# A graph layer on one core: x W1b + b1 read from a table in DRAM, both silus in one operation, source addresses made once and kept in DRAM, x once in SBUF, 72 and 76 columns a step

## The chip, the cores and the metric

The kernel runs on one core of a Trainium2 chip. A core has TensorE (PE), VectorE (DVE), ScalarE (ACT), GpSimd (POOL) and SyncE (SP), each with an instruction stream of its own, and sixteen DMA engines that they share. The streams meet at semaphores only. The metric is device time in microseconds, from the first to the last instruction of one execution and the little around it; the result is compared in runs of both kernels on the same chip.

An engine's stream is walked by its sequencer. It hands instructions to the engine, and carries out register loads (TENSOR_LOAD), semaphore instructions and DMA issues by itself. The profile counts only the engine's own work as busy.

## What is computed

One message-passing layer on a graph with 12,500 nodes of 64 features and 400,000 edges with 16 features. The edges are sorted by destination.

```
m_in = concatenate([x[src], x[dst], edge_attr])          # 400000 x 144
h = silu(m_in @ W1 + b1)                                 # 400000 x 64
messages = silu(h @ W2 + b2)                             # 400000 x 64
agg = segment_sum(messages, dst, 12500)                  # 12500 x 64
out = layernorm(x + silu(concatenate([x, agg]) @ W3 + b3))
```

W1 is used in three parts: W1a for x[src], W1b for x[dst], W1c for the edge features. All numbers are float32.

## The kernel before

**Tiles and steps.** Edges go in tiles of 128, eight tiles to a step ("oct"). There are 3125 tiles and NO = 391 steps (the loop at line 601 runs over o). TensorE packs two tiles, a pair, side by side: 64 features of one on partitions 0 to 63 and of the other on 64 to 127. The loop is emitted under a manual schedule, so the order of PE, ACT, DVE and SP is the order in which the lines are written. GpSimd's gathers are scheduled by their buffers alone, three steps ahead (AHEAD) with five buffers.

**x[src] W1a.** For the first 12 steps (RAW) GpSimd gathers rows of x. In these steps a table pa = x W1a is made in DRAM (`table`), and from then on GpSimd gathers its rows: one indirect DMA a tile (line 373), and an identity matmul turns each pair of gathered tiles and adds them to PSUM (line 454). Not every tile is gathered by GpSimd. There are two other ways:

- *Columns* (`columns`, lines 271 to 300). x lies transposed in SBUF (xs, 64 features by nodes, a copy in each half of the partitions). For some pairs, those at the steps in the list `pairs`, each edge's column of four bytes on 64 partitions is copied into a tile cx of 128 columns, and a matmul with w1d multiplies it (line 451). ScalarE copies ACOLS = (32, 28) columns a step and VectorE VCOLS = (32, 32), by a reduction over one element. The addresses are loaded into the engine's registers before (line 290), 16 at the start of each of the two parts and then 8 at a time, cut at tile borders. A pair takes 256 columns, and it spares GpSimd the first two gathers of its step.
- *Rows* (`rows`, line 324). SP issues 16 DMAs a step, each of one row of pa, into a tile rx. A tile pair is complete every 16 steps.

The addresses of columns come by a DMA of 256 indices of src (`index`, line 351, three steps ahead, three buffers cxi) and two operations of VectorE that turn them into byte addresses (`address`, line 359), one a half, since the two halves of xs differ in address.

**x[dst] W1b and edge features.** Edges of a tile go to at most 48 nodes in a row, a window (S = 48). SP loads the window of x for step o + 3 (line 392), TensorE multiplies it by W1b (`window_product`, line 397), VectorE writes it into one of three tiles xw by a mask (`window_copy`, line 402). The tile's last 32 rows hold W1c. VectorE compares destinations with node numbers (`compare_dst`, line 424, 96 rows of oh), below which the edge features lie, and one matmul of xw with oh adds both (line 441).

**The two layers.** `first_layer` ends with a silu of ScalarE over 128x512 with b1 as bias (line 458). `second_layer` of the step before adds b2 by a matmul of three rows, multiplies by W2 and ends with another silu (line 473). The columns of ScalarE stand in two parts ahead of the two silus. `add_up` (line 482) multiplies the messages by the comparison eh (`compare_nodes`, line 430), and `add_window` (line 487) of VectorE adds the result into agg, four steps later. A node group's end, W3, layernorm and store, is spread over the steps (`later`).

**VectorE's order in step o:** the window bases (every fourth step), add_window(o - 4), compare_dst(o + 1), its first 32 columns, window_copy(o + 1), compare_nodes(o + 1), its second 32 columns, now and then the address operations or parts of the node groups.

**SP's order in step o:** index(o + 3), the rows' index (every 16 steps), the destinations and edge features of the next three steps (every third step), the window for o + 3, then the 16 rows. A DMA that waits holds back those behind it.

Of the kernel before, what the change touches and what calls it, by code (L numbers as in the profile page):

```python
# [28 lines left out]
RAW = 12  # L29
TABLES = 7  # L30
ACOLS = (32, 28)
VCOLS = (32, 32)
ROWS = 16
LOADS = (16, 8)
XBASE = (0, 64 << 18)
XADDR = 36864
# [7 lines left out]
@with_exitstack  # L44
def kernel(
    ctx: ExitStack,
    tc: tile.TileContext,
    x: bass.AP,
    xt: bass.AP,
    src_c: bass.AP,  # L50
    src_row: bass.AP,
    dst_c: bass.AP,
    dst_row: bass.AP,
    attr_t: bass.AP,
    dst_2: bass.AP,
    attr_2: bass.AP,
    base: bass.AP,
    w1: bass.AP,
    b1: bass.AP,
    w2: bass.AP,  # L60
    b2: bass.AP,
    w3: bass.AP,
    b3: bass.AP,
    out: bass.AP,
    edges: int,
):

    nc = tc.nc
    N, D = x.shape  # L80

    const = ctx.enter_context(tc.tile_pool(name="const", bufs=1))
    dram = ctx.enter_context(tc.tile_pool(name="dram", bufs=1, space=DRAM))
    pa = dram.tile([N, D], F32, name="pa")
    badi = const.tile([1, 1], I32, name="badi")
    ident = const.tile([P, P], F32, name="ident")
    make_identity(nc, ident)

    with ExitStack() as inner:
        windows(inner, tc, ident, badi, pa, x, xt, src_c, src_row, dst_c, dst_row, attr_t, dst_2, attr_2, base, w1, b1, w2, b2, w3, b3, out, edges)  # L90

    flag = nc.values_load(badi[0:1, 0:1], min_val=0, max_val=2 * P,
                          skip_runtime_bounds_check_because="a count of partitions")
    with tc.If(flag > 0):
        general(tc, ident, x, xt, src_c, dst_c, dst_row, attr_t, w1, b1, w2, b2, w3, b3, out, edges)


def windows(ctx, tc, ident, badi, pa, x, xt, src_c, src_row, dst_c, dst_row, attr_t, dst_2, attr_2, base, w1, b1, w2, b2, w3, b3, out, edges):
# [33 lines left out]
    b1s = const.tile([P, 1], F32, name="b1s")  # L132
# [3 lines left out]
    for s in range(2):  # L136
        h = slice(s * D, (s + 1) * D)
        nc.scalar.dma_start(w1d[h, h], w1[0:D, :])
        nc.scalar.dma_start(b1s[h, :], b1.rearrange("(k o) -> k o", o=1))
# [3 lines left out]
    def resident(s, c):  # L143
        w = min(XC, NP - c)
        nc.scalar.dma_start(xs[s * D:(s + 1) * D, c:c + w], xt[:, c:c + w])

    resident(0, 0)
# [3 lines left out]
    resident(0, XC)  # L151
# [41 lines left out]

    bf = fast.tile([1, NO], F32, name="bf")
# [10 lines left out]
    nc.vector.memset(mask[:, :D], 0.0)  # L205
    nc.vector.memset(mask[:, D:], 1.0)
# [29 lines left out]
    for k in range(3):  # L236
        t = fast.tile([P, P], F32, name=f"xw{k}")
        nc.vector.memset(t, 0.0)
        for q in range(2):
            nc.sync.dma_start(t[E + q * A:E + (q + 1) * A, q * D:(q + 1) * D], w1[2 * D:2 * D + A, :])  # L240
        xw.append(t)
# [6 lines left out]
    with tc.tile_pool(name="gat", bufs=AHEAD + 2) as gat, tc.tile_pool(name="drp", bufs=2) as drp, \  # L248
# [4 lines left out]
            tc.tile_pool(name="ps2", bufs=2, space=PSUM) as ps2, \  # L253
# [17 lines left out]
        def columns(o, eng, part):  # L271
            if o < RAW:
                return
            lo = (o - RAW) * RATE
            if eng == ENG.Activation:
                lo, n = lo + sum(ACOLS[:part]), ACOLS[part]
            else:
                lo, n = lo + sum(ACOLS) + sum(VCOLS[:part]), VCOLS[part]
            hi, todo = lo + n, n
            while lo < hi:  # L280
                j, e0 = lo // (2 * P), lo % (2 * P)
                if j >= len(pairs):
                    return
                n = min(hi - lo, P - e0 % P, LOADS[lo > hi - todo])
                if pairs[j] not in cols:
                    cols[pairs[j]] = cx.tile([P, P], F32, name="cx")
                t = cols[pairs[j]].bitcast(U8)
                s = e0 // P
                h = slice(s * D, (s + 1) * D)
                _, regs = nc.values_load_multi_w_load_instructions(  # L290
                    indices[j][0:1, e0:e0 + n], engines=(eng,), min_val=XBASE[s] + XADDR,
                    max_val=XBASE[s] + XADDR + 4 * (N - 1), skip_runtime_bounds_check_because="src names a node")
                for e, r in zip(range(e0 % P, e0 % P + n), regs):
                    to, frm = t[h, 4 * e:4 * e + 4], xb[h, ds(r - (XBASE[s] + XADDR), 4)]
                    if eng == ENG.DVE:

                        nc.vector.tensor_reduce(to, frm[:, :, None], AX.X, OP.max)  # L297
                    else:
                        nc.scalar.copy(to, frm)  # L299
                lo += n  # L300
# [46 lines left out]
        def index(o):  # L347
            for j in begun(o):
                t = cxi.tile([1, 2 * P], I32, name="cxi")
                e = octs[pairs[j]][1] * P  # L350
                nc.sync.dma_start(t, src_row[:, e:e + 2 * P])
                indices[j] = t

        def address(o):
            for j in begun(o):
                t = indices[j]
                for s in range(2):
                    h = slice(s * P, (s + 1) * P)
                    nc.vector.tensor_scalar(t[:, h], t[:, h], 4.0, float(XBASE[s] + XADDR), op0=OP.mult, op1=OP.add)

# [25 lines left out]

        def window_load(o):
            if o % 4 == 0:
                bases(ENG.SP, o)
            xr = win.tile([D, 2, S], F32, name="xr")  # L390
            frm = xt[:, ds(winreg.pop((ENG.SP, o)), S)]
            nc.sync.dma_start(xr, frm[:, None, :].to_broadcast([D, 2, S]))
            winrow[o] = xr

        def window_product(o):
            pw = mis.tile([P, P], F32, name="mm")
            nc.tensor.matmul(pw[:E, :], winrow[o].rearrange("k s w -> k (s w)"), w1bb.rearrange("k s m -> k (s m)"),  # L397
                             start=True, stop=True)
            winrow[o] = pw

        def window_copy(o):
            nc.vector.tensor_tensor(xw[o % 3][:E, :], winrow.pop(o)[:E, :], mask[:E, :], op=OP.mult)  # L402

        def load(c, o0=0, o1=CT // OT):
# [6 lines left out]
            for k in range(2):  # L411
                nc.sync.dma_start(dr[k * S:(k + 1) * S, e], dst_2[k:k + 1, d].to_broadcast([S, e.stop - e.start]))
            nc.sync.dma_start(oh[E:, e], attr_2[:, d])

        hots = {}
# [18 lines left out]
        def first_layer(o):  # L434
# [5 lines left out]
            p1 = ps1.tile([P, OT // 2, P], F32, name="p1")  # L440
            nc.tensor.matmul(p1[:, :k], xw[o % 3], oh, start=True, stop=False, skip_group_check=True)  # L441
            if o < RAW:
# [4 lines left out]
                xg = work.tile([P, OT // 2, P], F32, name="m")  # L447
# [8 lines left out]
            columns(o, ENG.Activation, 0)  # L456
            h = work.tile([P, OT // 2, P], F32, name="h")
            nc.scalar.activation(h[:, :k], p1[:, :k], AF.Silu, bias=b1s)  # L458
            made[o] = h, eh

        def second_layer(o):
# [3 lines left out]
            h, eh = made.pop(o)  # L465
            p2 = ps2.tile([P, OT, D], F32, name="p2")
# [4 lines left out]
            columns(o + 1, ENG.Activation, 1)  # L471
            m = work.tile([P, OT, D], F32, name="m")
            nc.scalar.activation(m[:, :n2], p2[:, :n2], AF.Silu)  # L473
            made[o] = m, eh

        def add_up(o):
            c, t0, n, first, last = octs[o]
            m, eh = made.pop(o)
# [114 lines left out]
        tables = list(range(0, N, 8 * P))  # L593
        cuts = [SCT] + [min(t + 46 * OT, TILES) for t in range(SCT, TILES, 46 * OT)]
# [3 lines left out]
        with tc.manual_schedule(engines={ENG.PE, ENG.Activation, ENG.DVE, ENG.SP}):  # L598
            compare_dst(0)
            compare_nodes(0)  # L600
            for o in range(NO + 1):
# [3 lines left out]
                for k in parts[3 * o - 3:3 * o] if o else []:  # L605
                    n = min(XC, NP - k)
                    nc.scalar.activation(agg[:, k:k + n], zero.to_broadcast([P, n]), AF.Copy)
                if o < 2:
                    for c in parts[2:5] if o == 0 else parts[5:]:
                        resident(0, c)  # L610
# [10 lines left out]
                if 5 <= o < 5 + (len(parts) + 1) // 2:  # L621
                    for c in parts[(o - 5) * 2:(o - 4) * 2]:
                        resident(1, c)
# [10 lines left out]
                if o + 1 < NO:  # L634
                    window_product(o + 1)
# [7 lines left out]
                if o < NO:  # L643
                    first_layer(o)
                if o == 0:
                    nc.vector.tensor_copy(b2r, b2p[:, None, :].to_broadcast([3, OT, D]))
                if o + 1 < NO:
                    window_copy(o + 1)
# [11 lines left out]
                if o >= 1:  # L660
                    for c in tables[(o - 1) * per:o * per]:
                        table(c)
                if o >= 2:
                    add_up(o - 2)
                if o >= 1:
                    second_layer(o - 1)
                address(o + 2)
# [297 lines left out]
```

## Time and profile before

| | |
|---|---|
| median of 10 runs | 3433.37 us (3429.05 to 3437.4) |
| profiled execution, time | 3431.88 us |
| its span, first to last instruction | 3429.6 us |
| PE busy | 2567.5 us (75%) |
| DVE busy | 2513.8 us (73%) |
| ACT busy | 2724.4 us (79%) |
| POOL busy | 2566.8 us (75%) |
| granted clock of TensorE | 0.769 |

No engine is at 90%, and in the 40 slices of the span all four stand at 7 or 8 tenths from the third slice to the last but one. Busy shares alone don't say which engine sets the time. A row of the costliest groups reads: line, engine, operation, what it writes and reads, count; busy us and mean ns of one; then the idle time just before, and what ended most of it. "issue" there means that the engine waited for nothing that the profile shows: its sequencer was doing something else. The mean of a short instruction is longer than the distance to the next, since one begins before the other has ended.

In the chain of waits that ended last only the last 110 us are covered, so it does not tell of the steady part.

### The profile page before, as it was taken

To read this page: it belongs to the slowest core of one execution; us is meant where nothing else is said; L and a number is where in the kernel's file an instruction comes from. 1 tells how busy PE (TensorE), PEld (TensorE's weight loads), DVE (VectorE), ACT (ScalarE), POOL (GpSimd) and SP (SyncE) were. 2 spreads that over 40 slices of the span, in tenths; PEclk is the share of its full clock that TensorE was granted. 3 is DMA by queue.
4 is the path that set the end of the run, shared out by engine and by line. 5 is a ranking of instruction groups with operands and counts; after the bars stand their busy time and mean duration, and the time that the engine had idled before them with its cause. 6 is when DMAs were issued, how large, how long until landed. Compare 5 with 4: busy or idle time off the path is not lost. (4 is left out here: it accounts for less than half of the span.)

```text
span 3429.6 us, 107486 instructions
## 1 busy us (share of the span) xinstructions
PE 2567.5 (75%) x15131; PEld 1814.0 (53%) x15131; DVE 2513.8 (73%) x26395; ACT 2724.4 (79%) x23402; POOL 2566.8 (75%) x2724
## 2 busy tenths in 40 slices
PE   7877777777777777677777777777777767777776
PEld 5555555555555555455555555545555545455554
DVE  2477778777787777777778777777777777777774
ACT  2488879788788888887888878888888788788884
POOL 7777777777777777777777777777777777777774
PEclk8877778777777777877777777778767787777777
DMA  6532232323333323323333322332333332333232
GB/s 133 117 69 61 62 69 61 62 60 70 63 65 68 66 61 61 69 61 66 64 61 67 73 61 59 71 59 61 68 63 64 68 69 61 62 69 60 60 74 47
DMA packets 203943, 229.98 MB, mean 67 GB/s; under 512 B 133612, under 2 KB 141988, under 8 KB 202324
## 3 DMA queue, kind: packets, MB, share of 16 engines
q1 hardware_dynamic: 101528, 122.61, 15.9%
q0 software_dynamic: 86880, 89.14, 14.0%
q10 hardware_dynamic: 14812, 11.26, 1.4%
q14 instruction: 595, 4.87, 0.5%
q8 instruction: 128, 2.10, 0.3%
HBM read 216.36 MB, written 6.40 MB: 65 GB/s over the span
## 5 line engine op out<-in xcount | busy, mean ns | idle before, releaser
L373 POOL DMA_INDIRECT ga<-pa,sc x2619 | 2473.8, 945 | 798.8 <-issue 712.8
L299 ACT COPY cx<-xs 64x4 uint8 x22560 | 2217.3, 188 | 149.2 <-issue 122.7
L297 DVE TENSOR_REDUCE cx<-xs 64x4 uint8 x24032 | 1782.5, 150 | 541.9 <-issue 469.1
L454 PE MATMUL p<-ident,ga 128*128 128x128 f32 x2620 | 540.2, 344 | 393.2 <-DMA ga<-pa,sc 391.5
L441 PE MATMUL p<-oh,xw 128*128 128x512 f32 (+1 forms) x782 | 623.2, 890 | 224.7 <-DVE xw L402 223.9
L454 PEld LDWEIGHTS p<-ident,ga 128*128 128x128 f32 x2620 | 483.7, 251 | 578.5 <-issue 499.3
L469 PE MATMUL p<-w2d,h 128*128 128x128 f32 x3126 | 592.1, 348 | 0.0
L469 PEld LDWEIGHTS p<-w2d,h 128*128 128x128 f32 x3126 | 500.2, 243 | 114.2 <-issue 114.2
L458 ACT ACTIVATE h<-p,b1s 128x512 f32<-128x512 f32 x391 | 267.9, 685 | 352.3 <-PE p L454 291.8
L482 PE MATMUL pg<-eh,m 128*64 128x48 f32 x6250 | 315.9, 253 | 182.2 <-DVE agg L487 156.4
L482 PEld LDWEIGHTS pg<-eh,m 128*64 128x64 f32 x6250 | 267.4, 165 | 254.1 <-issue 131.5
L424 DVE TENSOR_TENSOR oh<-dr,wrow 96x512 f32<-96x512 int32 x391 | 264.3, 676 | 135.5 <-DMA dr<-in_dst 82.3
L441 PEld LDWEIGHTS p<-oh,xw 128*128 128x128 f32 x782 | 155.7, 249 | 319.6 <-DVE xw L402 278.6
L473 ACT ACTIVATE m<-p 128x512 f32<-128x512 f32 x391 | 231.4, 592 | 59.9 <-PE p L469 52.2
L397 PE MATMUL mm<-w1bb,xr 64*96 64x128 f32 x782 | 230.4, 385 | 37.9 <-DMA xr<-in_xt 26.2
L430 DVE TENSOR_TENSOR eh<-wrow,dc 128x384 f32<-128x384 f32 x391 | 211.7, 541 | 0.0
L397 PEld LDWEIGHTS mm<-w1bb,xr 64*96 64x96 f32 x782 | 122.1, 204 | 105.8 <-issue 48.6
L467 PE MATMUL p<-b2r,one 3*128 3x512 bf16 x391 | 176.8, 452 | 0.0
L451 PEld LDWEIGHTS p<-cx,w1d 128*128 128x128 f32 x364 | 98.1, 269 | 144.4 <-issue 144.4
L487 DVE TENSOR_TENSOR agg<-agg,pg 128x48 f32 x391 | 78.7, 201 | 116.7 <-PE mm L517 55.9
L402 DVE TENSOR_TENSOR xw<-mm,mask 96x128 f32<-96x128 f32 x391 | 109.4, 280 | 12.5 <-PE mm L397 6.6
L373 POOL DMA_INDIRECT ga<-in_x,sc x96 | 90.8, 946 | 30.5 <-issue 27.6
(81 smaller groups left out, 759.2 us busy)
## 6 DMA issues: line engine op xcount, KB each, us to landing
rx<-pa SPq DMA_DIRECT2D x5888, 0.2 KB
dr<-in_dst SPq DMA_DIRECT2D x260, 288.0 KB
ga<-pa,sc POOLq DMA_INDIRECT x2619
oh<-in_attr SPq DMA_DIRECT2D x130, 192.0 KB
xr<-in_xt SPq DMA_DIRECT2D x391, 24.0 KB
xs<-in_xt ACTq DMA_DIRECT2D x12, 512.0 KB
pa<-v ACTq DMA_DIRECT2D x12, 256.0 KB
xa<-in_x SPq DMA_DIRECT2D x24, 128.0 KB
```

Source lines behind the costliest of these rows:

```text
L297: nc.vector.tensor_reduce(to, frm[:, :, None], AX.X, OP.max)
L299: nc.scalar.copy(to, frm)
L373: nc.gpsimd.indirect_dma_start(out=ga[:, i, :], out_offset=None, in_=x if o < RAW else pa[:, :], in_offset=bass.IndirectOffsetOnAxis(ap=sc ...
L397: nc.tensor.matmul(pw[:E, :], winrow[o].rearrange("k s w -> k (s w)"), w1bb.rearrange("k s m -> k (s m)"), start=True, stop=True)
L424: nc.vector.tensor_tensor(oh[:E, :], dr[:, e:e + w], wn[:E, o:o + 1].to_broadcast([E, w]), op=OP.is_equal)
L430: nc.vector.tensor_tensor(eh[:, :n], row[:, None, :].to_broadcast([P, n, S]), rel[:, t0:t0 + n, None].to_broadcast([P, n, S]), op=OP.is_equal)
L441: nc.tensor.matmul(p1[:, :k], xw[o % 3], oh, start=True, stop=False, skip_group_check=True)
L454: nc.tensor.matmul(p1[:, i, :], g2.rearrange("p s d -> p (s d)"), ident, start=False, stop=(i == k - 1), skip_group_check=True)
L458: nc.scalar.activation(h[:, :k], p1[:, :k], AF.Silu, bias=b1s)
L469: nc.tensor.matmul(p2[:, 2 * i:2 * i + 2, :].rearrange("p s d -> p (s d)"), h[:, i, :], w2d, start=False, stop=(i == k - 1), skip_group_ch ...
L473: nc.scalar.activation(m[:, :n2], p2[:, :n2], AF.Silu)
L482: nc.tensor.matmul(pg[s * D:(s + 1) * D, :], m[:, i, :], eh[:, i, :], start=(i < 2), stop=(i >= n - 2), skip_group_check=True)
```

## The change

It does five things:

1. *Table for W1b.* A second table pw1b, of 128 columns, left half zero, right half x W1b + b1, is made in steps 8 to 57 (`table_b`: four matmuls, a copy of ScalarE, a DMA). From step 60 (OWN) SP loads xw from it by one DMA, in which rows 0 to 47 and 48 to 95 are shifted by 64 columns against each other. window_product and window_copy are left for the steps before; b1 is added there by a further matmul of one row. xw has five tiles instead of three. The halves of oh and of mask change places.
2. *One silu.* p1 of step o and p2 of step o - 1 lie in one PSUM tile of two banks, and one operation of ScalarE over 128x1024 does both (`silus`). It stands after first_layer(o) and second_layer(o - 1); both parts of ScalarE's columns stand before it. add_up(o - 2) moves behind it.
3. *Addresses once.* src is read once into agg's memory (before agg is cleared), made into byte addresses by one operation in step 1, and written to DRAM (adr). `index` loads from there. `address` goes.
4. *x once.* xs is filled on partitions 0 to 63 only; the columns of both halves are read from there.
5. *Columns.* ACOLS = (40, 32) and VCOLS = (40, 36); every register load is of eight at most.

```diff
-ACOLS = (32, 28)
-VCOLS = (32, 32)
+OWN = 60
+XWB = 5
+ACOLS = (40, 32)
+VCOLS = (40, 36)
-LOADS = (16, 8)
-XBASE = (0, 64 << 18)
-XADDR = 36864
+LOADS = 8
+XADDR = 37344
...
-    def resident(s, c):
+    def resident(c):
         w = min(XC, NP - c)
-        nc.scalar.dma_start(xs[s * D:(s + 1) * D, c:c + w], xt[:, c:c + w])
+        nc.scalar.dma_start(xs[:D, c:c + w], xt[:, c:c + w])
...
+    adr = dram.tile([1, TILES * P], I32, name="adr")
+    at = agg[:, :TILES].bitcast(I32)
+
+    def addresses_made():
+        nc.vector.tensor_scalar(at, at, 4.0, float(XADDR), op0=OP.mult, op1=OP.add)
+        nc.sync.dma_start(adr.rearrange("o (p j) -> (o p) j", p=P), at)
...
-                n = min(hi - lo, P - e0 % P, LOADS[lo > hi - todo])
+                n = min(hi - lo, P - e0 % P, LOADS)
...
-                    to, frm = t[h, 4 * e:4 * e + 4], xb[h, ds(r - (XBASE[s] + XADDR), 4)]
+                    to, frm = t[h, 4 * e:4 * e + 4], xb[:D, ds(r - XADDR, 4)]
...
-                nc.sync.dma_start(t, src_row[:, e:e + 2 * P])
+                nc.sync.dma_start(t, adr[:, e:e + 2 * P])
...
-        def address(o):
-            for j in begun(o):
-                t = indices[j]
-                for s in range(2):
-                    h = slice(s * P, (s + 1) * P)
-                    nc.vector.tensor_scalar(t[:, h], t[:, h], 4.0, float(XBASE[s] + XADDR), op0=OP.mult, op1=OP.add)
...
+        def table_b(c):
+
+            n = min(2 * P, NP - c)
+            k = (n + P - 1) // P
+            ps = mis.tile([P, 2, D], F32, name="mm")
+            t = pbs[c // (2 * P) % 2]
+            for i in range(k):
+                p = min(P, n - i * P)
+                nc.tensor.matmul(ps[:p, i, :], xs[0:D, c + i * P:c + i * P + p], w1ab[:, 1, :], start=True, stop=False)
+                nc.tensor.matmul(ps[:p, i, :], ones[:, :p], b1r[:, 0, :], start=False, stop=True)
+            if n == 2 * P:
+                nc.scalar.copy(t[:, :, D:], ps)
+                nc.scalar.dma_start(pw1b[c:c + n, :].rearrange("(i p) d -> p i d", p=P), t)
+                return
...
         def window_load(o):
             if o % 4 == 0:
                 bases(ENG.SP, o)
+            if o >= OWN:
+                v = pw1b[ds(winreg.pop((ENG.SP, o)), S), :]
+                v = bass.AP(tensor=v.tensor, offset=v.offset, ap=[[D, 2]] + list(v.ap))
+                nc.sync.dma_start(xw[o % XWB][:E, :], v)
+                return
...
-            columns(o, ENG.Activation, 0)
-            h = work.tile([P, OT // 2, P], F32, name="h")
-            nc.scalar.activation(h[:, :k], p1[:, :k], AF.Silu, bias=b1s)
-            made[o] = h, eh
...
-            columns(o + 1, ENG.Activation, 1)
-            m = work.tile([P, OT, D], F32, name="m")
-            nc.scalar.activation(m[:, :n2], p2[:, :n2], AF.Silu)
-            made[o] = m, eh
+        def silus(o):
+
+            pp = both.pop(o)
+            hm = outs.pop(o)
+            columns(o, ENG.Activation, 0)
+            columns(o, ENG.Activation, 1)
+            k = [-(-octs[q][2] // 2) if 0 <= q < NO else 0 for q in (o, o - 1)]
+            if k == [OT // 2, OT // 2]:
+                nc.scalar.activation(hm, pp, AF.Silu)
+            else:
+                for j in range(2):
+                    if k[j]:
+                        nc.scalar.activation(hm[:, j, :k[j]], pp[:, j, :k[j]], AF.Silu)
+            made[o] = hm[:, 0]
+            messages[o - 1] = hm[:, 1].rearrange("p i (s d) -> p (i s) d", s=2)
...
+                if o == 0:
+                    nc.sync.dma_start(at, src_row[:, :TILES * P].rearrange("o (p j) -> (o p) j", p=P))
...
-                if 5 <= o < 5 + (len(parts) + 1) // 2:
-                    for c in parts[(o - 5) * 2:(o - 4) * 2]:
-                        resident(1, c)
...
-                if o + 1 < NO:
+                if o + 1 < min(OWN, NO):
                     window_product(o + 1)
...
+                if o == 1:
+                    addresses_made()
...
+                if o + 1 < min(OWN, NO):
+                    window_copy(o + 1)
                 if o + 1 < NO:
-                    window_copy(o + 1)
                     compare_nodes(o + 1)
...
+                if o >= 1:
+                    second_layer(o - 1)
+                silus(o)
+                if 8 <= o < 8 + len(tables_b):
+                    table_b(tables_b[o - 8])
                 if o >= 2:
                     add_up(o - 2)
-                if o >= 1:
-                    second_layer(o - 1)
-                address(o + 2)
```

## The prediction

> **What bounds the kernel now.** I read first the costliest groups of the page, then the waits of GpSimd, then the timeline of VectorE in the steady part, and last the register loads of line 290.
>
> From the page, the costliest groups (line, engine, operation; then busy us, mean ns of one | idle time before and what ended it):
>
> ```profile
> L373 POOL DMA_INDIRECT ga<-pa,sc x2619 | 2473.8, 945 | 798.8 <-issue 712.8
> L299 ACT COPY cx<-xs 64x4 uint8 x22560 | 2217.3, 188 | 149.2 <-issue 122.7
> L297 DVE TENSOR_REDUCE cx<-xs 64x4 uint8 x24032 | 1782.5, 150 | 541.9 <-issue 469.1
> L424 DVE TENSOR_TENSOR oh<-dr,wrow 96x512 f32<-96x512 int32 x391 | 264.3, 676 | 135.5 <-DMA dr<-in_dst 82.3
> ```
>
> GpSimd gathers back to back. Its 2715 indirect DMAs (2619 and 96 early ones) start 1.249 us apart, 0.945 busy and 0.30 of issue; the first begins at 2.8 us, the last at 3394.4, and 2715 x 1.249 = 3391. What follows the last gather is some 35 us. So **POOL sets the time**: 6.94 gathers a step make 8.67 us.
>
> The waits of GpSimd say that nobody holds it up:
>
> ```profile
> POOL ga L373 <- issue: 740.4, 2427, 0.5
> POOL ga L373 <- DMA ga<-pa,sc: 61.3, 201, 0.3
> ```
>
> No wait is over 0.5 us, so neither a buffer nor an index was ever late. The next question is how much room VectorE and ScalarE have, which the change loads further. The timeline of VectorE, the second half of one step (start, us, engine, line):
>
> ```profile
> 2015.93 0.54 DVE L430 TENSOR_TENSOR eh<-wrow,dc 128x384 f32<-128x384 f32 x1
> 2016.39 0.58 DVE L297 TENSOR_REDUCE cx<-xs 64x4 uint8 x8
> 2017.13 0.62 DVE L297 TENSOR_REDUCE cx<-xs 64x4 uint8 x8 [0.15 <-issue]
> 2018.05 0.62 DVE L297 TENSOR_REDUCE cx<-xs 64x4 uint8 x8 [0.30 <-issue]
> 2018.97 0.62 DVE L297 TENSOR_REDUCE cx<-xs 64x4 uint8 x8 [0.30 <-issue]
> 2019.82 0.20 DVE L487 TENSOR_TENSOR agg<-agg,pg 128x48 f32 x1 [0.22 <-DVE cx L297]
> ```
>
> Eight columns take 0.62 us of the engine and then it stands still for 0.30 us, "issue". A block of eight is 0.92 us (2017.13, 2018.05, 2018.97). What fills the gap is in the answer on line 290 for the same stretch, the loads that fetch eight addresses into registers:
>
> ```profile
> L290 DVEq TENSOR_LOAD <-cxi x3: 595/596/598, 2016.4 to 2018.3; - x3
> ```
>
> A load of eight registers keeps VectorE's sequencer 0.596 us, and it then needs 0.32 us to hand out the eight reductions; the engine, at 64 ns a reduction, is done earlier. So **VectorE's columns are bound by the sequencer**, which its 73% busy does not show. Over the whole trace: 761 pairs of successive loads of eight with only columns between them start 0.918 us apart (median; 5th percentile 0.916; mean 0.947, since 7% hold a stall of 0.35 us). A load of 16 with its columns takes 1.665 (load 1.098), a load of 4 takes 0.62 (load 0.345).
>
> A step of VectorE now: two parts of 32 columns, each 16 + 8 + 8: 2 x (1.665 + 2 x 0.918) = 7.00; with the splits at tile borders the trace has 7.12 a step. Step length less this is 0.95 us in the median and 0.43 to 0.7 in the steps without waits. The shortest eight steps in a row take 7.69 each. So VectorE needs 7.7 to 7.9 of 8.67 us and has under 1 us of room.
>
> **The change, part by part.**
>
> *Columns, 60 to 72 and 64 to 76.* A step fetches 148 instead of 124, a pair of tiles is 256 columns, and the pairs of the run rise from 182 to 217 (the largest n with 12 + ceil(256n/148) + 1 below 390). Each pair spares two gathers: 2715 - 70 = 2645 gathers, 2645 x 1.249 = 3304 us. This alone would give -87 us.
>
> *Columns on VectorE.* Every load now takes eight, the first of a part too. 40 columns are 5 x 0.918 = 4.59; 36 are 4 x 0.918 + 0.62 = 4.29; splits add 0.05. Sum **8.93 us, against 7.12: +1.81 a step**. Twelve more columns are 12 x 0.115 = 1.4 of it; the rest is two loads of 16 that become four of 8. The blocks alone are longer than the step of 8.45 that 6.76 gathers allow.
>
> *window_copy and address.* From step 60 the xw multiply goes: 0.28 us of the engine, but on the sequencer it is one dispatch, 0.04. The two tensor_scalars per pair on the indices (364, mean 0.243) and their semaphore wait go: some 0.17 us of sequencer per pair, 0.08 a step. Both are engine time inside gaps that the sequencer makes, so I count 0.12. The remaining overhead of a step: add_window and oh 0.25, eh 0.04, base registers 0.09, stalls of 0.35 every 128 or so instructions 0.25, node work and other small things 0.05 = 0.68, which also fits the residue above. **Step of VectorE after: 8.93 + 0.65 = 9.55 to 9.6**, I take 9.55.
>
> The Trainium skill's page "Perfetto Trace Analysis", section "Optimizing Scalar/DVE Operations", puts the overhead of a small DVE operation on SBUF at about 60 ns. This trace agrees for the engine (64 ns from reduction to reduction), and by that rule 76 columns would be some 4.6 us, VectorE would stay far below 8.45, and the sum would be GpSimd's. The row decides, since it holds the loads as well.
>
> *ScalarE.* A copy is 93.4 ns engine-bound; a load of eight 0.547 plus 0.25 to hand out, a block 0.80 us. Nine blocks 7.2. The one silu over 1024 columns is not in the trace: with 512 it takes 0.592 without bias, with 384 0.491, so 0.79 ns a column and 1.00 us for 1024; at most 2 x 0.592 = 1.18. Taken 1.0. Sum: by the engine 72 x 0.0934 + 1.0 to 1.18 = 7.7 to 7.9, by the sequencer 7.2 + 0.25 of stalls + dispatches = 7.5. It is under VectorE, so costs nothing; without that cover it would still be under GpSimd's 8.45. The silu now waits for both layers. Behind it stand the next 72 copies and, in steps 8 to 57, the copy of the new table (0.26 by the row of 128x128) and its DMA issue (0.38 to 0.44). Who waits for it: second_layer and add_up on TensorE. After VectorE's columns end, TensorE needs 1.12 + 0.38 + 0.83 + 0.41 + 1.16 = 3.9 us for both layers (lines 441, 451, 454, 467 and 469 in the timeline of one step), silu 1.0, columns 7.2: 12.1 against the next inputs at 9.55 + 3.9 = 13.4. 1.3 us are left, and VectorE needs the sums four steps later.
>
> *TensorE* loses window_product from step 60 (0.46 us a step by the timeline); it is at 6.6 us a step; the two rows for b1 and the table's products come before. Nothing on the path.
>
> *Halves.* Copies that read partitions 0 to 63 and write 64 to 127 are not in the trace. The engine idles 0.30 to 0.41 us of each block of eight on VectorE, so up to 40 ns each are hidden; I take 0. On ScalarE 1.3 us over 72, 18 ns each.
>
> *SP.* xw comes by one DMA of 48 KB in place of xr's 24 KB (issue 0.62 us), the addresses come from DRAM in place of src_row at the same size. SP's step is 16 x 0.254 for rows, up to 1.42 for their registers, and about 1.3 more: 6.8, below 9.55. The new index of a pair is at the head of SP's step and waits until a tile three pairs back is read; behind it are dr, the attributes, xw and the rows. A pair now lasts 1.73 steps, not 2.06, so dr leaves 1.46 steps ahead of its comparison (14 us), not 2.13 (18). The longest wait for dr in the trace is 3.8 us, so I take 0.
>
> *Start.* Reading 1.6 MB of src, writing it back, against the second copy of x (3.2 MB) that goes: even, within 20 us. First columns remain at about 143 us (steps 0 to 11).
>
> **Sum.** 143 + 376 steps x 9.55 = 3591 + end. From the last column to the end of the span it is 49 us now, 13 of them for late gathers that will be early; I take 42. Span 3776, and 2 us more around it (3431.88 against 3429.6 in the profiled execution, which is 1.5 us under the median of the runs shown). **Forecast 3775 us, +10%.**
>
> **Rivals.**
> (1) *GpSimd stays the bound*, if the loads of registers hide behind the engine: 3304 + 38 = 3342 us, faster by 2.7%. For it: fewer gathers, no wait on POOL now. Against it: 0.916 to 0.918 in three quarters of 761 blocks is a rhythm, and no arrangement in the change moves a load ahead. It decides only where VectorE's step is under 8.45: with 9.5 blocks and 0.65 us beside them that is 0.82 us a block. Chance 0.07.
> (2) *VectorE's blocks alone*: all other work of its sequencer falls into waits. 143 + 376 x 8.93 + 42 + 2 = 3545. Against it: those dispatches are in the same sequencer. Chance 0.07.
> (3) *A new wait on top*: dr, or the index tile's three buffers, comes late by 3 us every third step, or ScalarE's loop closes: +1 us x 376, 4150. For it: SP's lead is shorter. Against: 14 us. Chance 0.08.
> (4) *ScalarE sets the step*, VectorE cheaper than thought: 8.7 a step by loads and waits, 143 + 3271 + 44 = 3458, the same within 1%. Chance 0.03.
>
> **How the numbers follow.** Forecast 0.75. Its own range is a step of 9.3 to 9.85: 3680 to 3890. With rival 2 taken in below, the range for 8 in 10 is 3540 to 3890. A measurement of this kernel tells 0.2% (7 us) from no change. Faster is rival 1 and a little of 4: 0.08; same 0.01; slower 0.91.
>
> **What would show it.** Right: POOL's idle time is no more all "issue" but waits for buffers (ga released by line 454's matmul); VectorE's reductions in blocks 0.92 apart through the step, its idle "issue" near 950 us; gathers 2645; columns on VectorE 28,500; waits of TensorE for ga gone, in their place waits for cx or oh of VectorE. Wrong: gathers still 1.249 apart without a break, or VectorE's blocks closer than 0.85 us.

## The result, and the profile after

The changed kernel takes 3908.48 us (median of 8 runs, 3902.61 to 3916.61), the kernel before 3432.91 beside it: ratio 1.1383, 95% interval 1.1373 to 1.1393. It is slower by 476 us. The forecast was slower, 3775 us with a range of 3540 to 3890, so the direction and what bounds it were right, and the size was 133 us short.

The costliest groups of the page after, the rows that answer to those shown of before:

```profile
L390 POOL DMA_INDIRECT ga<-pa,sc x2549 | 2412.5, 946 | 1315.1 <-issue 663.6
L324 ACT COPY cx<-xs 64x4 uint8 x27052 | 2700.9, 189 | 144.6 <-issue 119.6
L322 DVE TENSOR_REDUCE cx<-xs 64x4 uint8 x28500 | 2153.8, 141 | 902.4 <-issue 832.8
L524 ACT ACTIVATE hm<-p 128x1024 f32<-128x1024 f32 x389 | 397.3, 1021 | 318.6 <-PE p L513 315.4
L466 DVE TENSOR_TENSOR oh<-dr,wrow 96x512 f32<-96x512 int32 x391 | 264.5, 677 | 34.4 <-DMA dr<-in_dst 28.1
```

GpSimd has 70 gathers fewer (2549 and 96 early ones), and half of its idle time is no longer its own issue. Its waits say whose it is:

```profile
POOL ga L390 <- issue: 690.5, 2260, 0.6
POOL ga L390 <- PE p L498: 594.0, 220, 12.1
```

It stands 594 us until TensorE has turned an older gather and frees its buffer. It is ahead of the others now and no longer the bound. TensorE in turn waits for VectorE, whose add_window frees the sums that add_up writes:

```profile
PE pg L538 <- DVE agg L543: 1002.7, 301, 5.4
```

The clock granted to TensorE is lower too (0.702, before 0.769), but it doesn't make the loss: without the table (experiment 4) it is 0.751, and the steps after 60 take 9.74 us, not less than the 9.69 here. VectorE has 4468 columns more than before (28,500 against 24,032) and 832.8 us of idle time before them in place of 469.1. Its timeline, one step from add_window to the second comparison:

```profile
2006.78 0.20 DVE L543 TENSOR_TENSOR agg<-agg,pg 128x48 f32 x1
2006.90 0.68 DVE L466 TENSOR_TENSOR oh<-dr,wrow 96x512 f32<-96x512 int32 x1
2007.50 0.59 DVE L322 TENSOR_REDUCE cx<-xs 64x4 uint8 x8
2008.39 0.59 DVE L322 TENSOR_REDUCE cx<-xs 64x4 uint8 x8 [0.31 <-issue]
2009.31 0.59 DVE L322 TENSOR_REDUCE cx<-xs 64x4 uint8 x8 [0.33 <-issue]
2010.24 0.59 DVE L322 TENSOR_REDUCE cx<-xs 64x4 uint8 x8 [0.33 <-issue]
2011.15 0.59 DVE L322 TENSOR_REDUCE cx<-xs 64x4 uint8 x8 [0.32 <-issue]
2011.67 0.54 DVE L472 TENSOR_TENSOR eh<-wrow,dc 128x384 f32<-128x384 f32 x1
```

No wait on another engine shows in it. Five blocks of eight follow each other 0.89 to 0.93 us apart, with 0.31 to 0.33 of "issue" ahead of the last four. In the whole trace some 2140 pairs of successive loads of eight start 0.921 us apart in the median (0.918 before). The register loads behind the gaps:

```profile
L305 DVEq TENSOR_LOAD <-cxi x3809: 339/596/1084, 171.8 to 3871.2; - x191
```

There are 3809 of them instead of 2391, and the median is 0.596 us as before.

The time splits as follows. A step begins here with the register operation of VectorE's sequencer ahead of add_window; where add_window itself has to wait, it comes later (at step 12 after, at 171.8 us, not 166.7).

| stretch | before | after | forecast for after |
|---|---|---|---|
| to step 12 | 143 us | 167 us | 143 us |
| steps 12 to 60, each | 8.57 us | 11.02 us | 9.55 us |
| steps 60 to 388, each | 8.62 us | 9.69 us | 9.55 us |
| of these, without node work: median | 8.06 us | 9.49 us | |
| step 388 to the end of the span | 49 us | 36 us | 42 us |

The span is 3908.4 us, so 132 us are to be explained against the forecast's 3776: 24 at the start, 48 x 1.47 = 71 in steps 12 to 60, 328 x 0.14 = 45 later, and -6 at the end (the parts are rounded).

### The profile page after: what moved, and what is told of

Same layout as the page of the kernel before. It is cut to its first block, busy times and chain, and to the rows that moved or that the text cites. A ratio compares the mean times of both kernels' runs of the same rounds, so it can differ in the third digit from the quotient of the medians.

```text
span 3908.4 us, 116590 instructions
## 1 busy us (share of the span) xinstructions
PE 2709.2 (69%) x14985; PEld 1931.7 (49%) x14985; DVE 2750.4 (70%) x30173; ACT 3126.5 (80%) x27555; POOL 2506.6 (64%) x2654
## 4 chain that ended last, share of the span: by engine, by line
DVE 39%; issue 19%; SPq 13%; PE 8%; DMA 6%; DVEq 6%; ACT 6%; ACTq 1%
DVE cx L322 32%; SPq L348 7%; DVEq L305 6%; ACT cx L324 5%; SPq L344 3%; DVE eh L472 3%; DMA rx<-pa 3%; DVE oh L466 2%; PE p L485 2%; DMA xw<-pw1b 1%; SPq L429 1%; ACTq L305 1%; PE p L513 1%; DVE agg L543 1%; PE pg L538 1%
## 5 line engine op out<-in xcount | busy, mean ns | idle before, releaser
L324 ACT COPY cx<-xs 64x4 uint8 x27052 | 2700.9, 189 | 144.6 <-issue 119.6
L322 DVE TENSOR_REDUCE cx<-xs 64x4 uint8 x28500 | 2153.8, 141 | 902.4 <-issue 832.8
L538 PE MATMUL pg<-eh,hm 128*64 128x48 f32 x6250 | 381.0, 287 | 1016.9 <-DVE agg L543 1002.7
L538 PEld LDWEIGHTS pg<-eh,hm 128*64 128x64 f32 x6250 | 321.5, 197 | 1085.7 <-DVE agg L543 1062.0
L485 PE MATMUL p<-oh,xw 128*128 128x512 f32 (+1 forms) x782 | 761.5, 1075 | 4.3 <-DVE xw L444 2.5
L524 ACT ACTIVATE hm<-p 128x1024 f32<-128x1024 f32 x389 | 397.3, 1021 | 318.6 <-PE p L513 315.4
L513 PE MATMUL p<-w2d,hm 128*128 128x128 f32 x3126 | 513.1, 313 | 95.1 <-ACT hm L524 95.0
L513 PEld LDWEIGHTS p<-w2d,hm 128*128 128x128 f32 x3126 | 435.3, 216 | 225.8 <-ACT hm L524 117.5
L495 PE MATMUL p<-cx,w1d 128*128 128x128 f32 x434 | 132.2, 406 | 0.0
L438 PE MATMUL mm<-w1bb,xr 64*96 64x128 f32 x120 | 36.9, 400 | 56.7 <-DVE xw L444 33.4
```

Source lines behind the costliest of these rows:

```text
L485: nc.tensor.matmul(p1[:, :k], xw[o % XWB], oh, start=True, stop=False, skip_group_check=True)
L513: nc.tensor.matmul(p2[:, 2 * i:2 * i + 2, :].rearrange("p s d -> p (s d)"), h[:, i, :], w2d, start=False, stop=(i == k - 1), skip_group_ch ...
L524: nc.scalar.activation(hm, pp, AF.Silu)
L538: nc.tensor.matmul(pg[s * D:(s + 1) * D, :], m[:, i, :], eh[:, i, :], start=(i < 2), stop=(i >= n - 2), skip_group_check=True)
```

## The experiments

All ratios are against the kernel before, run on the same chip.

**1. The changed kernel with the old columns.**

```diff
-ACOLS = (40, 32)
-VCOLS = (40, 36)
+ACOLS = (32, 28)
+VCOLS = (32, 32)
```

> The changed kernel with the old numbers of columns (32, 28 and 32, 32), loads of eight kept. Theory, VectorE's register loads and the columns that they feed set the step: two parts of four blocks of 0.92 us and 0.62 to 0.7 beside them make 8.1 us, below the 8.67 of GpSimd's 6.94 gathers, so GpSimd is the bound again: 3430 to 3480 us, what is over 3430 coming from the first 60 steps. Rival, the new structure (table, one silu, columns read across the halves of the partitions) is what costs: over 3700 us with the old columns too.

Measured: 3613.29 us, ratio 1.052 (1.048 to 1.056). It lies between the two theories. 295 of the 476 us go with the columns, so they are the greater part, but GpSimd isn't the bound again: 8.97 us a step after step 60 where its gathers need 8.67. The waits of TensorE in this run name something else:

```profile
PE p L485 <- DMA oh<-in_attr: 187.4, 78, 4.8
```

TensorE waits 78 times for the edge features, and VectorE (154.1 us, 70 times) for the destinations that are sent just before them, every third step. SP, which sends them, in the same run:

```profile
2073.11 0.79 SPq L454 DMA_DIRECT2D dr<-in_dst  x2
2074.00 0.37 SPq L455 DMA_DIRECT2D oh<-in_attr  x1
2074.56 0.70 SPq L429 DMA_DIRECT2D xw<-pw1b  x1
2076.99 5.98 SPq L348 DMA_DIRECT2D rx<-pa  x16
2083.09 0.23 SPq L375 DMA_DIRECT2D cxi<-adr  x1
```

Between the window and the rows 1.7 us go for the row addresses (the register load takes 1.50 in the mean and isn't shown in a timeline); otherwise SP goes from one issue to the next. Over steps 60 to 388 SP's instructions, with the gaps of up to 0.15 us between them, fill some 8.4 of the 8.97 us. In the rest it waits, most often at a row for an earlier DMA to land. SP is nearly full. Experiments 5 and 6 put that to the test.

**2. The kernel before with the new columns alone.**

```diff
-ACOLS = (32, 28)
-VCOLS = (32, 32)
+ACOLS = (40, 32)
+VCOLS = (40, 36)
```

> The kernel before with nothing but 72 and 76 columns (loads of 16 at the start of a part, then 8). Theory: VectorE's blocks are 1.665 + 3 x 0.918 and 1.665 + 2 x 0.918 + 0.62 = 8.54 us, with splits and the 0.75 beside them 9.35 a step: 143 + 376 x 9.35 + 40 = 3700 us (3650 to 3760). Rival, the columns by themselves are nearly free and fewer gathers win: under 3450 us.

Measured: 3785.03 us, ratio 1.102 (1.099 to 1.105). The columns alone make 352 us. The median of all steps is 9.41 us against the 9.35 expected, the mean 9.59 with the steps that also carry node work. The total is above the range of 3650 to 3760. The rest of the change isn't needed for this part of the loss.

**3. The changed kernel with loads of 16.**

```diff
-LOADS = 8
+LOADS = 16
```

> The changed kernel with loads of 16 registers throughout, where it had 8. Theory: a block of 16 is 1.665 us against 2 x 0.92, so VectorE's parts are 4.25 and 3.95, the step 8.85 instead of 9.56; steps 12 to 60, which ScalarE paces, gain little: 3908 - 0.7 x 328 = 3680 us (3640 to 3740). Rival, the engine's own work or a wait on another engine sets the step, and the size of a load does not matter: 3880 to 3910 us.

Measured: 3699.91 us, ratio 1.078 (1.073 to 1.082). A single number that alters nothing of what is computed, nor one instruction of the engine proper, gives 209 us back. The median of all steps is 8.85, as expected. VectorE's timeline:

```profile
2003.71 0.56 DVE L472 TENSOR_TENSOR eh<-wrow,dc 128x384 f32<-128x384 f32 x1
2004.56 1.11 DVE L322 TENSOR_REDUCE cx<-xs 64x4 uint8 x16 [0.29 <-issue]
2006.22 1.36 DVE L322 TENSOR_REDUCE cx<-xs 64x4 uint8 x20 [0.56 <-issue]
2007.61 0.21 DVE L543 TENSOR_TENSOR agg<-agg,pg 128x48 f32 x1
```

Sixteen columns are 1.66 us (2004.56 to 2006.22) where two blocks of eight were 1.84. ScalarE's loads grew as well, but there it saves nothing: a block of 16 is 1.596 us, two of eight are 1.602. Steps 12 to 60 stay at 11.1 us: something else paces them.

**4. The changed kernel without the table.** The window is multiplied and masked to the end.

```diff
-OWN = 60
+OWN = 1000
...
-                if 8 <= o < 8 + len(tables_b):
+                if False:
                     table_b(tables_b[o - 8])
```

> The changed kernel without the table of x W1b + b1: windows are multiplied and copied as in the first 60 steps to the end. Theory: steps 12 to 60 take 11.0 us instead of 9.7 because ScalarE copies the table and issues its DMA there (silu 1.02, copy 0.25, issue 0.38, restart 1.06, 72 copies at 0.10 = 9.9, and the shared PSUM buffers); without it they fall to 9.7, -62 us; the copy of the window on VectorE costs one dispatch of 0.04 us in 331 steps, +13: 3860 us (3840 to 3875). Rival A, these steps are slow for another reason: 3905 to 3930. Rival B, the window copy costs VectorE its 0.28 us a step: 3940.

Measured: 3860.94 us, ratio 1.124 (1.119 to 1.130). Steps 12 to 60 fall from 11.02 to 9.82, later ones rise from 9.69 to 9.74: window_copy costs VectorE's sequencer one dispatch, not its 0.28 us. The start is shorter in this execution too (step 12 at 151 us, not 167).

**5. Old columns and no table**, the edits of 1 and 4 together.

> The changed kernel with the old columns (32, 28 and 32, 32; loads of eight) and without the table: what is left of the change is one silu, addresses made once, x once and b1 by a matmul. The old columns with the table took 3613 us, 9.0 us a step where GpSimd allows 8.67, and TensorE waited there for edge features that SP had sent late. Theory: SP is nearly full (16 row DMAs 5.4, their registers 1.3, the window 0.62 and the rest make some 8.4 a step in the kernel before), and the table pushes it over (registers 1.48, the load of xw and the wait for its landing); without the table SP is as before, and GpSimd's 2715 gathers set the end: 3435 to 3475 us. Rival, one silu or columns across the halves cost: over 3560.

Measured: 3448.37 us, ratio 1.0045 (1.0025 to 1.0065). GpSimd is the bound again (8.67 us a step), and the register load of the rows is back at 1.30 us from 1.48. One silu, x once, columns read across the halves, addresses made once and b1 by a matmul together cost some 15 us here, and gain nothing.

**6. Old columns, the table kept, 8 rows a step.**

```diff
-ROWS = 16
+ROWS = 8
```

> The changed kernel with the old columns, the table kept, and 8 rows a step by SP instead of 16. GpSimd gets 24 gathers more: 2739 x 1.249 = 3421. Theory, SP's own instructions made the 9.0 us: SP has 2.7 us more room, GpSimd sets the end, 3421 + 36 + 30 to 60 for the start and the table: 3490 to 3520 us. Rival, the latency of the transfers or ScalarE's loop in the first 60 steps and after makes the 9.0 us: 3600 us or more, as with 16 rows.

Measured: 3488.1 us, ratio 1.016 (1.013 to 1.019). That is 2 us under the expected range. With 24 gathers more the kernel is 125 us faster than with 16 rows, and SP's own instructions fill some 5.2 of 8.60 us a step. So the rows that SP issues made the 9 us of experiment 1.

**7. A piece of the table sent one step later.**

```diff
+        unsent = []
         def table_b(c):
...
-                nc.scalar.dma_start(pw1b[c:c + n, :].rearrange("(i p) d -> p i d", p=P), t)
+                unsent.append((pw1b[c:c + n, :].rearrange("(i p) d -> p i d", p=P), t))
...
             columns(o, ENG.Activation, 0)
+            while unsent:
+                nc.scalar.dma_start(*unsent.pop(0))
             columns(o, ENG.Activation, 1)
```

The table is used from step 64 here.

> The changed kernel, but a piece of the table is sent one step after it was copied, between the two parts of ScalarE's columns (the table is used from step 64). Theory: in steps 12 to 60 ScalarE's sequencer stands at the DMA issue until the copy before it has ended, and its next register load comes only then (1.06 us idle after each issue); with the issue moved, ScalarE's step is 1.02 + 0.25 + 7.3 and some 0.4 = 9.0, under VectorE's 9.6, and the steps fall from 11.0 to 9.8 us: 3908 - 55 = 3853 us (3840 to 3870). Rival, the shared PSUM buffers or the table's matmuls on TensorE hold these steps: 3890 to 3910.

Measured: 3892.09 us, ratio 1.134 (1.130 to 1.137): the rival's number. Steps 12 to 60 take 10.76 us. That the issue stands behind the copy is not the cause. ScalarE stands still before its columns between 166 and 660 us as long as in the changed kernel (98.6 us, shown below):

```profile
ACT cx L324 <- issue: 106.9, 59, 8.6
```

**8. The addresses of a pair loaded one step ahead, not three.**

```diff
-                index(o + 3)
+                index(o + 1)
```

> The changed kernel, the addresses of a pair loaded one step ahead instead of three. Theory: in steps 12 to 60 SP stands at the head of its step until ScalarE, which has 9.9 us of work there, has read the index tile three pairs back; the destinations behind it are then late for VectorE, and the step is 11.0. With the load two steps later that tile has long been read: steps 12 to 60 fall to some 10.0 us, the later ones stay at 9.7, which are VectorE's: 3908 - 48 = 3860 us (3840 to 3880). Rival, TensorE's and ScalarE's shared PSUM buffers hold these steps: 3890 to 3910.

Measured: 3911.74 us, ratio 1.139 (1.137 to 1.141). Nothing is gained, and steps 12 to 60 take 11.25 us. SP's wait at the index tile is not the cause by itself.

After both misses I read ScalarE in such a step of the changed kernel again, with the register loads and semaphore waits that are not in a timeline:

```profile
429.94 1.02 ACT L524 ACTIVATE hm<-p 128x1024 f32<-128x1024 f32 x1
430.86 0.26 ACT L415 COPY pbs<-mm 128x128 f32<-128x128 f32 x1
435.49 0.38 ACTq L416 DMA_DIRECT2D pw1b<-pbs  x1
436.52 4.91 ACT L324 COPY cx<-xs 64x4 uint8 x48 [5.40 <-issue]
```

The copy ends at 431.1 us, but the piece is sent at 435.49, and no register load passes it: ScalarE is idle for 5.4 us. The instruction before the issue is a wait on a DMA semaphore, let go at 435.43. SP's row DMAs use that semaphore in turn; one of them, issued at 434.02, landed at 435.41. It is the fourth row of its step, and SP's timeline shows why it was late: the window's load and 1.4 us of register load for the rows stand before it.

```profile
430.82 0.61 SPq L433 DMA_DIRECT2D xr<-in_xt  x1
433.01 5.11 SPq L348 DMA_DIRECT2D rx<-pa  x16
```

So ScalarE waits, 4.3 us after its copy has ended, for a DMA that has nothing to do with its own, only because the two share a semaphore.

**9. The table sent by GpSimd's queue**, whose DMAs use other semaphores.

```diff
-                nc.scalar.dma_start(pw1b[c:c + n, :].rearrange("(i p) d -> p i d", p=P), t)
+                nc.gpsimd.dma_start(pw1b[c:c + n, :].rearrange("(i p) d -> p i d", p=P), t)
...
-                nc.scalar.dma_start(pw1b[c + i * P:c + i * P + p, :], t[:p, i, :])
+                nc.gpsimd.dma_start(pw1b[c + i * P:c + i * P + p, :], t[:p, i, :])
```

> The changed kernel, the pieces of the table sent by GpSimd's queue instead of ScalarE's. What the trace shows of steps 12 to 60: the issue of a table piece on ScalarE waits for a semaphore that SP's DMAs use in turn with it, and is let go when a row DMA of SP, issued late, has landed (435.43 us, with the row landing at 435.41 and the copy done at 431.1); no copy and no register load passes it. SP in turn waits for ScalarE to read index tiles, and so on round. GpSimd's DMAs use semaphores of their own, and it has 1.1 us a step to spare. Theory, this coupling is what makes 11.0 out of 9.7: steps 12 to 60 fall to 9.8, 3908 - 55 = 3850 us (3835 to 3870). Rival, the shared PSUM buffers, the copy or the matmuls of the table hold these steps: 3890 to 3910, as with the issue moved by a step (3892) and with the index loaded later (3912).

Measured: 3869.97 us, ratio 1.128 (1.125 to 1.130). The waits of ScalarE before its columns between 166 and 660 us, in the changed kernel:

```profile
ACT cx L324 <- issue: 98.6, 58, 6.8
```

and in this one:

```profile
ACT cx L324 <- issue: 12.2, 40, 0.6
```

Steps 12 to 60 fall from 11.02 to 10.24 us: 48 x 0.78 = 38 us, what the total shows. The issue on ScalarE was the larger part of the 71 us, but the theory's 9.8 isn't reached. What holds the other 0.4 us a step (20 us, against 9.82 without the table) wasn't tried. The trace has a candidate: between 166 and 660 us ScalarE's copy waits six times, 16.0 us in all, until an earlier piece of the table has landed.

**10. A version from the theory, in the new structure**: experiment 4's edit, VCOLS = (32, 32), LOADS = 16.

> A version made from the theory: no table, ScalarE 72 columns, VectorE 64, loads of 16. 199 pairs, 2681 gathers x 1.249 = 3349. VectorE: 4 x 1.665 + 0.1 + 0.75 = 7.5 us a step, ScalarE 7.2 + 1.02 = 8.2, GpSimd 8.56, SP some 8.5. Theory: GpSimd is the bound, 3349 + 36 + up to 40 = 3385 to 3430 us, at or a little under the kernel before. Rival, SP has no room below 8.7 us a step: 3440 to 3480 us.

Measured: 3453.34 us, ratio 1.0053 (1.0040 to 1.0065), the rival's range. The start is again late (step 12 at 160 us) and the step is 8.70, not 8.56.

**11. Old columns, no table, and addresses for each pair** by VectorE as before, so that agg can be cleared at once (to experiment 5, x once kept):

```diff
-                nc.sync.dma_start(t, adr[:, e:e + 2 * P])
+                nc.sync.dma_start(t, src_row[:, e:e + 2 * P])
...
+                nc.vector.tensor_scalar(t, t, 4.0, float(XADDR), op0=OP.mult, op1=OP.add)
...
-                    nc.sync.dma_start(at, src_row[:, :TILES * P].rearrange("o (p j) -> (o p) j", p=P))
...
-                    addresses_made()
```

> The changed kernel with old columns and without the table (3448 us), and now addresses made for each pair on VectorE as before. What is left of the change is one silu, x once, and b1 by a matmul. Theory: GpSimd sets the end, and the 12 us that it lost came in the first twelve steps, where agg can't be cleared before src has been read into it, made into addresses and written out; without that step 12 begins at some 145 us instead of 155: 3448 - 10 = 3438 us (3432 to 3444). Rival, the start is slow for one silu's sake: 3446 to 3452.

Measured: 3448.78 us over ten runs that spread from 3432.65 to 3477.74; ratio 1.0025 (1.0006 to 1.0044). Inconclusive: four of them lie below 3434 us, and its profiled execution, the longest, reaches step 12 at 171 us with no address made ahead. So a start as late as this doesn't need the addresses.

**12. The kernel before with other numbers**: loads of 16, ScalarE 72 columns, VectorE 64, six index tiles.

```diff
-ACOLS = (32, 28)
+ACOLS = (40, 32)
-LOADS = (16, 8)
+LOADS = (16, 16)
...
-            tc.tile_pool(name="cx", bufs=4) as cx, tc.tile_pool(name="cxi", bufs=3) as cxi, \
+            tc.tile_pool(name="cx", bufs=4) as cx, tc.tile_pool(name="cxi", bufs=6) as cxi, \
```

> The kernel before with loads of 16 throughout, ScalarE 40 and 32 columns, VectorE 32 and 32, and six index tiles instead of three. 199 pairs, 2681 gathers x 1.249 = 3349 us. VectorE 7.5 us a step, ScalarE 72 x 0.0934 + 1.28 and some 0.2 = 8.2, SP 8.3 to 8.5, GpSimd 8.56. Theory: GpSimd is still the bound and the start is as before: 3349 + 38 + 0 to 25 = 3387 to 3412 us, faster by 1%. Rival, SP with 8.4 us of its own work can't follow 8.56 without waits, as in the version with the new structure (3453): 3425 to 3460.

Measured: 3418.96 us, ratio 0.9946 (0.9929 to 0.9964): half a per cent, 16 us, faster than the kernel before beside it, less than the 1% hoped for and between the two ranges. GpSimd has 34 gathers fewer, worth 42 us, and spends more than half of that in steps of 8.63 us where its gathers allow 8.56 and in a few longer waits.

## Why the prediction was right and where it fell short

*What would bound it: right.* "Step of VectorE after: 8.93 + 0.65 = 9.55 to 9.6" measured 9.49 in the median of the steps without node work. The 3809 loads are 3316 of eight and 493 of four; at the prediction's own prices that is 8.93 a step, as forecast, and what is left of a step is 0.60 in the median, beside 0.65. Experiments 2 and 3 show that neither the engine nor fewer gathers decide, but the size and number of register loads. Two roundings of the sum go the same way: 8.93 + 0.65 is 9.58, of which 9.55 was taken (11 us over 376 steps), and 3776 + 2 is 3778, not 3775.

*The signs.* GpSimd's waits for a buffer, the 2645 gathers, the 28,500 columns and the blocks 0.92 apart came as named; VectorE's idle "issue" is 833 us, not near 950. One was wrong: TensorE was to wait for cx or oh of VectorE, and it waits for add_window (1002.7 us); for oh it waits 1.8 us.

*GpSimd's gain: right as a count*, 2645 gathers, and worth nothing, since it waits. Rival 1 fell with the 0.921.

*Node work: mis-sized.* "node work and other small things 0.05". Twenty of the 328 steps after step 60 hold a group's statistics and take 11.75 us on average, 28 with divisions take 10.0. Together (20 x 2.26 + 28 x 0.51) / 328 = 0.18 us a step over the 9.49. That is 0.13 above the term, most of the +0.14. When GpSimd was the bound this lay in the room that VectorE had; when VectorE is the bound, each microsecond of it counts whole.

*ScalarE in steps 8 to 57: the step that failed.* The prediction priced "the copy of the new table (0.26 by the row of 128x128) and its DMA issue (0.38 to 0.44)" and said of ScalarE "it is under VectorE, so costs nothing". The durations were right (0.26 and 0.38 in the trace) but the issue's waits were left out: it stops the sequencer until the copy is done, and until an unrelated DMA of SP has landed. ScalarE stood still for 98.6 us there, 2 us a step beside 8.4 us of work, more than VectorE's 9.8 us a step without the table could cover. Experiment 4 shows 58 us from the table in these steps, experiment 9 shows 38 of them to come with the queue that sends it; how the other 20 come about stays open. The remaining 13 of the 71 are there without the table too (9.82 against 9.55). Rival 3 had named a ScalarE loop, at 0.08, but spread it over all 376 steps.

*The start: mis-sized.* "even, within 20 us" came to 24 late. Without the table step 12 came at 151 to 171 us (experiments 4, 5, 10, 11), with it at 157 to 167, one profiled execution each, so a part of the table in it isn't shown. It lay as late without addresses made ahead (experiment 11). What makes it so uneven stays open.

*One silu: right.* 1.02 us measured, 1.00 taken.

*SP: wrong, without effect on the forecast.* "16 x 0.254 for rows" took the issue (0.225) and the register move (0.029) and left out what lies between: a row every 0.323 us in the median, 0.34 on average before. SP's own instructions filled some 8.2 of 8.62 us a step, not 6.8. Under VectorE's 9.5 it didn't show; in experiment 1 it did.

*Halves: right.* The block of eight kept its length (0.921 against 0.918), and ScalarE's too (0.801 against 0.802).

## What to carry to other kernels

Where many small instructions take their addresses from registers, cost them by the distance from one register load to the next, not by the engine's busy time: here a VectorE 73% busy had no room for 12 columns, and the size of a load alone was worth 209 us. Before an engine is given more, ask which others stand just under the bound (here VectorE and SP both) by the best steps, not by the mean, in which waits for the bound hide. A DMA issue on a busy engine is to be priced with all that it waits for, the DMA whose semaphore it reuses among them; the queue is chosen by that as well.

## What the runs showed of the hardware

A register load took 0.345 us for 4 registers, 0.596 for 8 and 1.098 for 16 on VectorE, about 63 ns a register. What is left of a block of eight, 0.918 - 0.596 = 0.322 us, is 40 ns a reduction; that nothing is handed to the engine during a load is read from this rhythm. Once in 112 to 128 instructions, or in a multiple of that, a block of eight took 0.35 us longer: 7% of the blocks. What the time goes to isn't shown. In these kernels the DMAs of SP and ScalarE took the same eight semaphores in turn, and each waited for the one before on its semaphore to land: a wait of 4.3 us on ScalarE for a row of 256 bytes.
